# A sparse graph attention kernel: part of the single-edge product moved from VectorE to ScalarE

## The chip, the cores and the metric

The kernel runs on one core of a Trainium2 chip as one program. The metric is the device time of that program in microseconds (us). A core has five engines that run side by side, each through its own queue of instructions in order: TensorE (PE; its weight loads are shown as PEld), VectorE (DVE), ScalarE (ACT), GpSimd (POOL) and SyncE (SP). An instruction that must wait for another engine holds up everything behind it in its own queue.

## The reference

Four graph layers over 3327 nodes with 512 features and a random, sparse adjacency matrix; each adds to its input `x` a layer of the normalized input `h = relu(layernorm(x))`. Layers 0, 2 and 3 are graph attention with 8 heads of 64, layer 1 is a mean over neighbours with linear maps. Layer 3, cut to what matters (0 and 2 differ in normalization and the last function):

```python
hp = jnp.einsum('nd,hdf->hnf', h, W)                     # per head
f_src = jnp.einsum('hnf,hf->hn', hp, a_src)
f_dst = jnp.einsum('hnf,hf->hn', hp, a_dst)
e = jax.nn.leaky_relu(f_src[:, :, None] + f_dst[:, None, :], 0.2)
e = jnp.where(adj[None] > 0, e, -9e15)
out = jnp.einsum('hij,hjf->hif', jax.nn.softmax(e, axis=-1), hp)
x = x + elu(out)                                          # layer 0: batch norm and relu
```

## The kernel before

The kernel first turns the adjacency matrix into lists of neighbours, then runs four stages one after another. The three attentions share the function `attend`. It works through 52 groups of 64 target nodes, two groups to a block of 128. The blocks are taken from both ends of the list, so a block of heavy groups is followed by a block of light ones (`ls.order`).

For each node of a table, one row holds the 8 heads' projected values, each of 64 numbers and a factor (65 in all, already scaled by an exponential), and 8 more numbers T. The softmax is taken apart so that the weight of an edge is max(r, T), with r from the target and T from the source; no exponential is left in the loop.

`PLAN` (line 53) says for each group how many chunks of 128 source rows it has: dense and mixed ones, in which each source may have many targets of the group, and chunks of single edges, in which each of the 128 rows belongs to one edge. `Lists.units` (line 585) cuts these into units: up to two chunks (`SLOTS`) for the first kind, up to three (`UNIT`) for single edges. A group with six chunks of single edges has two units of three, one with five a unit of three and one of two, one with four two of two, one with three a single unit of three. The plan has 7 groups with six, 10 with five, 21 with four and 14 with three.

Work of a unit of slots: VectorE makes `mx` (the maximum, line 1581) and `wgt` (times the mask, line 1585), of 128 x 1024 for two chunks; TensorE multiplies `wgt` with the rows into the accumulator `facc` (line 1616).

Work of a unit of single edges, chunk by chunk: TensorE picks r of each edge's target (`r_of`, `pick`, line 1515) with a matrix of edges; VectorE sums its three parts (`summed`, line 1523), takes the maximum with T (line 1568) and multiplies all rows of the unit by the weights into `vw` (line 1571: 128 x 1560 for three chunks, 128 x 1040 for two). TensorE multiplies `vw` with a matrix of ones and zeros, `ones_of`, into `facc` (line 1605), chunk by chunk, with the `pick` of a later unit after the first chunk.

ScalarE's work in `attend`, in the order of its queue at unit i:
- `early(i)`: in attention 0 it copies the turned edge matrix to `edges` (`kept`, line 1502), on which a later `pick` waits, and makes masks out of bits that VectorE has cut out (`on`, line 1461): `mask` for the next unit, if that is one of slots (line 1483), and `ones_of` with its mask (lines 1478, 1479) for a unit of single edges further on. In attentions 2 and 3 it only casts `ones_of` (line 1481).
- `later()`: the generators of groups that have ended go one step each. In this order, a step per unit: ScalarE copies `facc` to `sums` (line 1419); VectorE takes the reciprocal `rd` (line 1425); ScalarE multiplies eight heads' parts by it (line 1432, eight instructions, into `bn_y` in attention 0 and `fhp` in the others). In attentions 2 and 3, after the second group of a block, `fin_e` and `fin_x` follow on ScalarE (lines 1656, 1658) and two instructions on VectorE (lines 1662, 1663). In attention 0 the sums of the batch norm run beside: GpSimd subtracts (`bn_d`, line 1715), ScalarE squares (line 1711), TensorE adds up.

TensorE, VectorE and ScalarE keep the order in which the code issues their instructions (`manual_schedule`); GpSimd, which gathers the rows (line 1342), is ordered by the scheduler. `vw` has 2 buffers in attention 0 and 3 in the others, the gathered rows `rows_e` 5 and 6, `facc` 2.

Of the kernel before, what the change touches and what calls it, by code (L numbers as in the profile page):

```python
# [23 lines left out]
F32 = mybir.dt.float32  # L24
# [9 lines left out]
ALU = mybir.AluOpType  # L34
# [5 lines left out]
P = 128  # L40
H = 8
F = 64
# [28 lines left out]
UNIT = 3  # L71
# [1233 lines left out]
def sparse(ctx: ExitStack, tc: tile.TileContext, t: dict, out: bass.AP, WA, ls, cs, idx, rdeg, bias, wx_dram, first):  # L1305
# [5 lines left out]
    nc = tc.nc  # L1311
# [35 lines left out]
    def attend(layer, table, r_dram, r3, finish, tick=lambda: None, home=None, beside=None, edges=None):  # L1347
# [14 lines left out]
        with tc.tile_pool(name=f"fatt{layer}", bufs=2) as ap, tc.tile_pool(  # L1362
            name=f"facc_ps{layer}", bufs=2, space=PSUM
        ) as aps, tc.manual_schedule(engines={ET.PE, ET.DVE, ET.Activation}):
            loaded, ones_of, st_of, found, w_of, rrs, rbs, accs, ends, over = {}, {}, {}, {}, {}, {}, {}, {}, [], []
            ahead = 2

            def fetch(j):
                if j < len(groups):
                    rr = ap.tile([2, H * GB], F32, name="r_two", tag="r_two", bufs=2)  # L1370
                    nc.sync.dma_start(rr, r_dram[groups[j], :, :, :].rearrange("t h i -> t (h i)"))
                    rrs[j] = rr

            def spread(j):


                if j < len(groups):
                    rb = aps.tile([P, H * GB], F32, name="r_bc", tag="r_bc", bufs=1)
                    nc.tensor.matmul(rb, ones[0:2, :].bitcast(F32R), rrs.pop(j).bitcast(F32R), start=True, stop=True)
                    rbs[j] = rb.rearrange("p (h i) -> p h i", i=GB)  # L1380
# [57 lines left out]
            def later():  # L1438
                for e in list(ends):
                    if next(e, 0) == 0:  # L1440
                        ends.remove(e)
                tick()

            def load(i):

                if i < len(units):
                    _, _, e, rows, _, _, _, _ = units[i]
                    if e:
                        gi = ap.tile([P, UNIT, width], I32, name="rows_e", tag="rows_e", bufs=5 if layer == 0 else 6)
                    else:  # L1450
                        gi = ap.tile([P, SLOTS, width], I32, name="rows_s", tag="rows_s", bufs=4 if layer == 0 else 5)
                    loaded[i] = gi
                    take(gi, table, rows)
# [31 lines left out]
            def turned(i):  # L1485

                if layer == 0 and i < len(units) and units[i][2]:
                    _, g, _, rows, _, _, _, _ = units[i]
                    u = g % PG
                    mine = slice(u * GB, (u + 1) * GB)  # L1490
                    st = st_of[i] = aps.tile([P, UNIT, P], F32, name="st_ps", tag="st_ps", bufs=1)
                    for k in range(len(rows)):
                        nc.tensor.matmul(st[mine, k, :], ones_of[i][:, k, :], cs["ident"], start=True, stop=True)
# [12 lines left out]
            def pick(i):  # L1506

                if i < len(units) and units[i][2]:
                    _, g, _, rows, s0, _, _, _ = units[i]
                    b, u = divmod(g, PG)  # L1510
                    mine = slice(u * GB, (u + 1) * GB)
                    st = st_of.pop(i) if layer == 0 else edges[mine, s0 : s0 + len(rows), :]
                    re = found[i] = aps.tile([P, UNIT, 3 * H], F32, name="r_of", tag="r_of", bufs=1)
                    for k in range(len(rows)):
                        nc.tensor.matmul(re[:, k, :], st[:, k, :], r3[mine, b, :], start=True, stop=True)  # L1515

            def summed(i):

                if i < len(units) and units[i][2]:
                    n, re = len(units[i][3]), found.pop(i)  # L1520
                    mx = aps.tile([P, SLOTS, H, GB], F32, name="w_of", tag="mx", bufs=1)
                    w = w_of[i] = mx[:, 0, :UNIT, :H]
                    nc.vector.tensor_reduce(w[:, :n], re[:, :n].rearrange("p k (t h) -> p k h t", h=H), AX.X, ALU.add)  # L1523
# [8 lines left out]
            def due(i):  # L1532

                return [k for k in range(max(i + 1, 0), i + ahead + 2) if k < len(units) and k - lead[k] == i]

            def early(i):

                for k in due(i - 1):
                    kept(k)
                for k in due(i):  # L1540
                    masks(k, bits(k))

            def parts(i):

                if layer == 2 and i < EPARTS:
                    for u in range(PG):
                        mine = slice(u * GB, (u + 1) * GB)
                        cut = slice(i * ls.used[u] // EPARTS, (i + 1) * ls.used[u] // EPARTS)
                        nc.sync.dma_start(edges[mine, cut, :], edges_dram[mine, cut, :])
# [10 lines left out]
            for i, (j, g, e, rows, s0, begins, stops, last_slots) in enumerate(units):  # L1560
                n, m0 = len(rows), rows[0][0]
                gt = loaded.pop(i).bitcast(F32)
                T = gt[:, :n, H * (F + 1) : ROW]
                load(i + AHEAD)
                parts(i + 1)
                if e:
                    w = w_of.pop(i)
                    nc.vector.tensor_tensor(w[:, :n], w[:, :n], T, ALU.max)
                    vw = ap.tile([P, UNIT, H, F + 1], F32, name="vw", tag="vw", bufs=2 if layer == 0 else 3)
                    full = [P, n, H, F + 1]  # L1570
                    nc.vector.tensor_tensor(  # L1571
                        vw[:, :n],
                        gt[:, :n, : H * (F + 1)].rearrange("p k (h x) -> p k h x", x=F + 1),
                        w[:, :n].unsqueeze(3).to_broadcast(full),
                        ALU.mult,
                    )
                else:
                    mk = mask[:, m0 : m0 + n, :]
                    full = [P, n, H, GB]
                    mx = aps.tile([P, SLOTS, H, GB], F32, name="mx", tag="mx", bufs=1)  # L1580
                    nc.vector.tensor_tensor(  # L1581
                        mx[:, :n], rbs[j].unsqueeze(1).to_broadcast(full), T.unsqueeze(3).to_broadcast(full), ALU.max
                    )
                    wt = ap.tile([P, SLOTS, H, GB], F32, name="wgt", tag="wgt", bufs=2 if layer == 0 else 3)
                    nc.vector.tensor_tensor(wt[:, :n], mx[:, :n], mk.unsqueeze(2).to_broadcast(full), ALU.mult)  # L1585
                summed(i + 1)
                early(i)
                if begins:
                    fetch(j + 2)
                    acc = aps.tile([P, BANK], F32, name="facc", tag="acc")  # L1590
                    accs[g] = acc

                def others():
                    pick(i + ahead)
                    if last_slots:
                        spread(j + 1)

                for k in range(n):
                    if k == 1:
                        others()  # L1600
                    f, l = begins and k == 0, stops and k == n - 1
                    if e:
                        by = vw[:, k].rearrange("p (q v) x -> p v q x", v=PG)
                        for v in range(PG):
                            nc.tensor.matmul(  # L1605
                                accs[g][v * GB : (v + 1) * GB, :sw].rearrange("p (q x) -> p q x", x=F + 1),
                                ones_of[i][:, k, :],
                                by[:, v],
                                start=f,
                                stop=l,  # L1610
                            )
                        continue
                    for q in range(hq):
                        for v in range(PG):
                            h = q * PG + v
                            nc.tensor.matmul(  # L1616
                                accs[g][v * GB : (v + 1) * GB, q * (F + 1) : (q + 1) * (F + 1)],
                                wt[:, k, h, :],
                                gt[:, k, h * (F + 1) : (h + 1) * (F + 1)],
                                start=(f and q == 0),  # L1620
                                stop=(l and q == hq - 1),
                            )
                if n == 1:
                    others()
                ones_of.pop(i, None)
                for k in due(i):
                    turned(k)
                later()
                if stops:
                    ends.append(ending(g))  # L1630
# [353 lines left out]
```

## Time and profile before

| | |
|---|---|
| device time, median of 4 runs | 2322.55 us (2319.12 to 2326.47) |
| the profiled execution: time, span of the trace | 2328.36 us, 2326.6 us |
| busy: PE, PEld | 1854.1 us (80%), 1044.1 us (45%) |
| busy: DVE, ACT, POOL | 1703.4 us (73%), 1100.0 us (47%), 1153.2 us (50%) |
| DMA | 561.86 MB, 241 GB/s on average |
| `vw` of attentions 0, 2 and 3: first and last | 370.6 and 2304.0 us |
| instructions of line 1571 | 270: 114 of 128 x 1560, 156 of 128 x 1040 |

A row of the profile names the line, the engine, the operation, what it writes and reads, its shape and its count, then busy us and the mean ns of one. In a list of waits, "A <- B" says that A's engine sat idle until B was done; the last numbers are the us in total, the times and the longest. A timeline row starts with its start and its length in us; in brackets stands the idle time ahead of it and what ended it. Neighbouring small instructions of one engine overlap in part, so the distance from start to start, not the length, is what one costs. Lines are those of the kernel before unless said otherwise.

### The profile page before, as it was taken

The page shows a single profiled execution, that of the slowest core. Times are in us where ns is not written, and L with a number is a line of the kernel's source. Part 1 is how long each engine was busy: PE and PEld are TensorE (multiplying, and loading weights), DVE is VectorE, ACT ScalarE, POOL GpSimd, SP SyncE. Part 2 cuts the span into 40 slices and gives each one's busy share as a digit, 9 for nine tenths or more (in the row PEclk, how much of TensorE's full clock was granted, in tenths as well). Part 3 has the DMA queues.
Part 4 walks back from the last instruction along what each step waited for, and adds up shares of the span by engine and source line. Part 5 has one row for each costly group of instructions (what it writes and reads, how often), then busy time and mean ns, then how long its engine had stood idle before and what let it go on. Part 6 is the DMA issues. An engine that isn't in the chain of part 4 may idle for free. (4 is left out here: it accounts for less than half of the span.)

```text
span 2326.6 us, 42809 instructions
## 1 busy us (share of the span) xinstructions
PE 1854.1 (80%) x14843; PEld 1044.1 (45%) x14843; DVE 1703.4 (73%) x3056; ACT 1100.0 (47%) x4124; POOL 1153.2 (50%) x1205
## 2 busy tenths in 40 slices
PE   4899576777888599899999857888888767777775
PEld 3655244454555244233333345555444444444442
DVE  5466977998889890255555568888777659999996
ACT  3566112555666553223333204678886713444544
POOL 0000024668777200677777356655555136776772
PEclk9789777999999899999999958998997967887777
DMA  8687157897889473888888698877777358888883
GB/s 312 248 289 278 33 198 264 291 297 245 272 263 297 146 276 114 270 256 258 267 263 257 195 299 252 263 231 242 243 244 224 104 220 270 261 285 264 281 279 112
DMA packets 204943, 561.86 MB, mean 241 GB/s; under 512 B 36985, under 2 KB 42745, under 8 KB 201392
## 3 DMA queue, kind: packets, MB, share of 16 engines
q0 software_dynamic: 93120, 327.86, 45.3%
q1 hardware_dynamic: 111600, 231.20, 28.6%
q8 instruction: 120, 1.97, 0.4%
q14 instruction: 103, 0.84, 0.1%
HBM read 496.07 MB, written 62.86 MB: 240 GB/s over the span
## 5 line engine op out<-in xcount | busy, mean ns | idle before, releaser
L1342 POOL DMA_INDIRECT rows_e<-table,idx x654 | 625.4, 956 | 670.4 <-DMA rows_s<-table 326.1
L1605 PE MATMUL facc<-vw,ones_of 128*64 128x260 f32 x2616 | 447.1, 457 | 84.8 <-DVE vw L1571 68.4
L1616 PE MATMUL facc<-rows_s,wgt 128*64 128x65 f32 x7200 | 351.7, 251 | 195.1 <-DVE wgt L1585 133.7
L1616 PEld LDWEIGHTS facc<-rows_s,wgt 128*64 128x64 f32 x7200 | 297.6, 160 | 302.6 <-DVE wgt L1585 162.6
L1571 DVE TENSOR_TENSOR vw<-rows_e,w_of 128x1040 f32<-128x1040 f32 (+1 forms) x270 | 395.7, 1466 | 9.3
L1342 POOL DMA_INDIRECT z_rows<-z_dram,idx x291 | 278.9, 959 | 231.3 <-DMA z_dram<-z_out 132.2
L1342 POOL DMA_INDIRECT rows_s<-table,idx x219 | 210.0, 959 | 212.9 <-PE facc L1616 134.5
L1581 DVE TENSOR_TENSOR mx<-r_bc,rows_s 128x1024 f32<-128x1024 f32 (+1 forms) x255 | 280.5, 1100 | 41.5 <-DMA rows_s<-table 27.8
L1432 ACT ACTIVATE fhp<-sums,rd 64x64 f32<-64x64 f32 x816 | 215.6, 334 | 185.7 <-DVE rd L1425 182.6
L1585 DVE TENSOR_TENSOR wgt<-mx,mask 128x1024 f32<-128x1024 f32 (+1 forms) x255 | 280.3, 1099 | 25.5 <-ACT mask L1483 9.0
L1605 PEld LDWEIGHTS facc<-vw,ones_of 128*64 128x64 f32 x2616 | 195.0, 156 | 223.1 <-issue 90.0
L1866 PE MATMUL sage_acc<-z_rows,z_mask 128*64 128x512 f32 x622 | 164.2, 604 | 14.3 <-DMA z_rows<-z_dram,idx 13.4
L1817 DVE TENSOR_TENSOR s_o<-n_ps,sage_b 128x512 f32<-128x512 f32 x26 | 18.0, 692 | 167.2 <-PE n_ps L1814 167.2
L1849 ACT CAST z_mask<-mask 128x128 f32<-128x128 uint8 (+1 forms) x201 | 51.2, 287 | 161.1 <-PE sage_acc L1866 158.6
L1419 ACT COPY sums<-facc 128x260 f32<-128x260 f32 x153 | 56.2, 367 | 136.7 <-PE facc L1605 135.6
L739 PE MATMUL wh_ps<-fWt,hT 128*128 128x512 f32 x208 | 115.5, 707 | 0.0
L1523 DVE TENSOR_REDUCE w_of<-r_of 128x16 f32<-128x48 f32 (+1 forms) x270 | 61.4, 227 | 65.8 <-PE r_of L1515 40.3
L1432 ACT ACTIVATE bn_y<-sums,rd 64x64 f32<-64x64 f32 x408 | 107.7, 334 | 2.6 <-DVE rd L1425 1.0
L1814 PE MATMUL n_ps<-fWx,bn_y 128*128 128x512 f32 x208 | 97.4, 611 | 0.0
L1866 PEld LDWEIGHTS sage_acc<-z_rows,z_mask 128*64 128x64 f32 x622 | 45.7, 137 | 115.0 <-issue 82.7
L921 PE MATMUL p_wh<-fWt,hT 128*128 128x512 f32 x208 | 96.1, 606 | 0.3 <-ACT hT L916 0.3
L1789 PE MATMUL z_ps<-fWx,bn_y 128*128 128x512 f32 x208 | 95.8, 606 | 0.6 <-ACT bn_y L1784 0.6
(252 smaller groups left out, 2832.0 us busy)
## 6 DMA issues: line engine op xcount, KB each, us to landing
adj_i<-in_adj SPq DMA_DIRECT2D x26, 1664.0 KB
rows_s<-table SPq DMA_DIRECT2D x46, 528.0 KB
table<-v_row SPq DMA_DIRECT2D x78, 264.0 KB
rows_s<-table SPq DMA_DIRECT2D x62, 264.0 KB
rows_s<-table SPq DMA_DIRECT2D x23, 632.0 KB
fin_x<-fx SPq DMA_DIRECT2D x52, 256.0 KB
rows_e<-table,idx POOLq DMA_INDIRECT x654
rows_s<-table SPq DMA_DIRECT2D x31, 316.0 KB
```

The costliest lines, as they stand in the source:

```text
L739: nc.tensor.matmul(wh, hT[:, kc, :], self.Wt[:, kc, :], start=(kc == 0), stop=(kc == KC - 1))
L921: nc.tensor.matmul(wh, hT[:, kc, :], self.Wt[:, kc, :], start=(kc == 0), stop=(kc == KC - 1))
L1342: nc.gpsimd.indirect_dma_start(out=dst, out_offset=None, in_=src[:, :], in_offset=bass.IndirectOffsetOnAxis(ap=idx[:, k : k + 1], axis=0))
L1432: nc.scalar.mul(hp[o0 : o0 + GB, h * F : (h + 1) * F], sm[mine, q, 0:F], rd[mine, q, :])
L1571: nc.vector.tensor_tensor(vw[:, :n], gt[:, :n, : H * (F + 1)].rearrange("p k (h x) -> p k h x", x=F + 1), w[:, :n].unsqueeze(3).to_broadca ...
L1581: nc.vector.tensor_tensor(mx[:, :n], rbs[j].unsqueeze(1).to_broadcast(full), T.unsqueeze(3).to_broadcast(full), ALU.max)
L1585: nc.vector.tensor_tensor(wt[:, :n], mx[:, :n], mk.unsqueeze(2).to_broadcast(full), ALU.mult)
L1605: nc.tensor.matmul(accs[g][v * GB : (v + 1) * GB, :sw].rearrange("p (q x) -> p q x", x=F + 1), ones_of[i][:, k, :], by[:, v], start=f, stop=l,
L1616: nc.tensor.matmul(accs[g][v * GB : (v + 1) * GB, q * (F + 1) : (q + 1) * (F + 1)], wt[:, k, h, :], gt[:, k, h * (F + 1) : (h + 1) * (F + 1)],
L1789: nc.tensor.matmul(ps, y[:, c, kc * P : (kc + 1) * P], Wx[:, 1, kc, :], start=(kc == 0), stop=(kc == KC - 1))
L1814: nc.tensor.matmul(ps, y[:, b, kc * P : (kc + 1) * P], Wx[:, 0, kc, :], start=(kc == 0), stop=(kc == KC - 1))
L1866: nc.tensor.matmul(acc[u * GB : (u + 1) * GB, :], m, z, start=f, stop=l)
```

## The change

In attentions 0 and 3, in a unit with three chunks of single edges, VectorE takes the maximum of the third chunk by itself into a new tile `w_last` (128 x 8, two buffers), then the maximum and the product of the first two chunks as before. ScalarE multiplies the third chunk's rows by the weights, head by head: eight instructions of 128 x 65, each with a column of `w_last` as its factor per partition. They stand ahead of `early(i)` and `later()` of the unit in ScalarE's queue. Units with two chunks and all units of attention 2 stay as they were. The file grows by two lines, so lines behind the change have numbers higher by two.

```diff
                 if e:
-                    w = w_of.pop(i)
-                    nc.vector.tensor_tensor(w[:, :n], w[:, :n], T, ALU.max)
+                    w, d = w_of.pop(i), n - (layer != 2 and n == UNIT)
+                    if d < n:
+                        ws = ap.tile([P, H], F32, name="w_last", tag="w_last")
+                        nc.vector.tensor_tensor(ws, w[:, d], T[:, d], ALU.max)
+                    nc.vector.tensor_tensor(w[:, :d], w[:, :d], T[:, :d], ALU.max)
                     vw = ap.tile([P, UNIT, H, F + 1], F32, name="vw", tag="vw", bufs=2 if layer == 0 else 3)
-                    full = [P, n, H, F + 1]
-                    nc.vector.tensor_tensor(
-                        vw[:, :n],
-                        gt[:, :n, : H * (F + 1)].rearrange("p k (h x) -> p k h x", x=F + 1),
-                        w[:, :n].unsqueeze(3).to_broadcast(full),
-                        ALU.mult,
-                    )
+                    full = [P, d, H, F + 1]
+                    V = gt[:, :n, : H * (F + 1)].rearrange("p k (h x) -> p k h x", x=F + 1)
+                    if d < n:
+                        for h in range(H):
+                            nc.scalar.mul(vw[:, d, h, :], V[:, d, h, :], ws[:, h : h + 1])
+                    nc.vector.tensor_tensor(vw[:, :d], V[:, :d], w[:, :d].unsqueeze(3).to_broadcast(full), ALU.mult)
```

## The prediction

> **What bounds the kernel now.** I read the page's slices first: in attention 0 and attention 3 VectorE (DVE) is the fullest engine. I then asked for the busy time of each engine in a stretch of each (columns: stretch, length, busy us of PE, PEld, DVE, ACT and POOL with instruction counts, granted TensorE clock, DMA share, GB/s).
>
> ```profile
> 365.00:790.00 425.00, 335.66 (x3850) 216.53 (x3851) 378.33 (x643) 247.00 (x827) 291.29 (x298) 0.96 0.83 267
> 1910.00:2306.00 396.00, 296.87 (x3327) 186.78 (x3325) 371.25 (x524) 172.48 (x586) 259.23 (x270) 0.80 0.83 261
> ```
>
> VectorE is busy 378 of 425 us and 371 of 396 us; ScalarE (ACT) 247 and 172. So VectorE sets the pace and ScalarE has room on average. What it waits for counts as much as its room. From the waits of ScalarE in 350 to 785 us and, below, in 1880 to 2310 us (who <- for whom: us, times, longest):
>
> ```profile
> ACT mask L1483 <- DVE on L1461: 86.3, 38, 12.4
> ```
>
> ```profile
> ACT fhp L1432 <- DVE rd L1425: 172.1, 50, 6.1
> ```
>
> ScalarE idles because VectorE has not yet written what it reads. It can't use that room for anything that also starts from a VectorE result of the same unit; the new work does exactly that.
>
> **What the change removes and adds.** By the plan, 7 groups have six chunks of single edges (two units of three), 10 have five (3+2), 14 have three: 14 + 10 + 14 = 38 units of three per attention, 76 in the two. The groups, shapes kept apart:
>
> ```profile
> L1571 DVE TENSOR_TENSOR vw<-rows_e,w_of 128x1560 f32<-128x1560 f32 x114 | 202.8, 1779 | 3.9
> L1571 DVE TENSOR_TENSOR vw<-rows_e,w_of 128x1040 f32<-128x1040 f32 x156 | 192.9, 1237 | 5.4
> L1432 ACT ACTIVATE bn_y<-sums,rd 64x64 f32<-64x64 f32 x408 | 107.7, 334 | 2.6 <-DVE rd L1425 1.0
> ```
>
> *VectorE.* The product goes from 1560 to 1040 elements: 1.779 - 1.237 = 0.54 us less. The maximum for 128x8 is new; the nearest small independent rows, a reduction at 2062.09 and a reciprocal at 2062.22, start 0.13 us apart. Net 0.41 us per unit, 38 x 0.41 = 15.6 us per attention, 31 us if every microsecond counted. Bounds: 0.54 (the new maximum free) to 0.32 (it costs the 0.22 us by which a dependent maximum holds back the product, 2062.34 to 2062.56), so 24 to 41 us in all.
>
> *ScalarE.* Eight scalings of 128x65 with a per-partition factor. The nearest row is L1432, also SBUF to SBUF with such a factor: eight in a row take 2.14 us (0.267 us from start to start). The other near row, L987 (128x64, from PSUM), takes 1.74 us for eight at 1446.99 and 1.67 at 1460.96. I take 2.15, keep 1.7 as the low bound and 8 x 0.334 = 2.67 (no overlap) as the high one. 38 x 2.15 = 82 us per attention: 329 of 425 and 254 of 396. Room on average.
>
> The Trainium skill, "ScalarE: Activation LUTs", section "What ACT_TABLE_LOAD costs", gives an ACTIVATE with one pointer operand 186 + 93 + 0.833 N ns, 93 ns of it overlapped back to back; for N = 65 that would be an estimated 0.24 us each and 1.92 us a unit. The same page, "Rules for kernel authors", speaks against the change: plain multiplies belong on VectorE. By that rule alone the total would rise; the busy rows above, with VectorE the full engine, say the opposite.
>
> *Order.* In the changed kernel's instruction order nothing else moves, except a few of POOL's gathers past each other and past its bn_d subtractions. TensorE waits for ScalarE only at the third chunk's matmuls. But the scalings stand at the start of a unit in ScalarE's queue. Behind them stand: the copy of edges (L1502) that TensorE's pick waits for between its chunks; the mask (L1483) that wgt of a following unit of slots waits for; eight L1432 of an earlier group; the copy of sums (L1419) that VectorE's reciprocal rd waits for; and in attention 3 fin_e and fin_x, which L1662 waits for. VectorE runs in order, so each of these, if late, stops it.
>
> **Walks.** I moved the rows of the timeline by hand: the third chunk's 0.41 us off VectorE, 2.15 us into ScalarE from 0.1 us after the new maximum, in the changed order. Attention 0, the worst group (six chunks), VectorE and then ScalarE before:
>
> ```profile
> 432.81 0.19 DVE L1568 TENSOR_TENSOR w_of<-w_of,rows_e 128x24 f32<-128x24 f32 x1
> 433.03 1.78 DVE L1571 TENSOR_TENSOR vw<-rows_e,w_of 128x1560 f32<-128x1560 f32 x1
> ...
> 435.33 0.18 DVE L1568 TENSOR_TENSOR w_of<-w_of,rows_e 128x24 f32<-128x24 f32 x1
> 435.55 1.78 DVE L1571 TENSOR_TENSOR vw<-rows_e,w_of 128x1560 f32<-128x1560 f32 x1
> ...
> 439.10 1.22 DVE L1585 TENSOR_TENSOR wgt<-mx,mask 128x1024 f32<-128x1024 f32 x1 [0.42 <-ACT mask L1483]
> ```
>
> ```profile
> 435.44 0.36 ACT L1478 ACTIVATE ones_of<-on 128x192 f32<-128x192 uint16 x1 [3.30 <-DVE on L1461]
> ...
> 436.10 2.13 ACT L1432 ACTIVATE bn_y<-sums,rd 64x64 f32<-64x64 f32 x8
> 438.26 0.47 ACT L1502 CAST edges<-st_ps 64x384 bf16<-64x384 f32 x1
> 438.75 0.31 ACT L1483 ACTIVATE mask<-on 128x128 uint8<-128x128 uint16 x1
> ```
>
> After: scalings 433.0 to 435.15, ones_of and its copy to 435.9, the eight L1432 to 438.05, the second unit's scalings to 440.2, edges to 440.7, mask to 441.0. VectorE, 0.8 us ahead, is ready for wgt at about 438.2 and gets it at 441.05: 2.9 us idle, 1.95 us later than now. Not all are like this. From 392 to 505 us (20 units of three) I find, in the change of VectorE's clock: groups of six -0.3, +0.3, +1.85, +0.95, 0, +1.45, 0; the three pairs of three-chunk groups between them 0 (+0.1, -0.1, 0): together **+4.2 us**. The other 18 units: pairs of three-chunk groups again 0; of the five-chunk groups four walked (521, 531, 565 and 589 us) give 0, +1, 0, 0, since rd already waits for sums there; +1 for all. Attention 0: **+5**.
>
> Attention 3 has no masks to make, so ScalarE's queue is shorter. The place that hurts is the second of two three-chunk groups (VectorE's rows, then ScalarE's, now):
>
> ```profile
> 1986.37 0.19 DVE L1568 TENSOR_TENSOR w_of<-w_of,rows_e 128x24 f32<-128x24 f32 x1
> ...
> 1990.88 0.17 DVE L1425 RECIPROCAL rd<-sums 128x4 f32<-128x4 f32 x1
> ```
>
> ```profile
> 1986.45 2.14 ACT L1432 ACTIVATE fhp<-sums,rd 64x64 f32<-64x64 f32 x8 [4.58 <-DVE rd L1425]
> 1988.61 0.38 ACT L1419 COPY sums<-facc 128x260 f32<-128x260 f32 x1
> ```
>
> Now sums is ready 1.9 us before rd. After, scalings (2.15), eight L1432 (2.15) and sums (0.4) end 4.9 us after the new maximum; VectorE reaches rd 4.1 us after it: 0.9 us idle, at six such pairs 5.4 us. The eight L1432 between two units of scalings, with fin behind, hold VectorE at L1662 1.8 us at 2003.48 and 0.4 at 2037.36: 2.2. The last pair ends the kernel: fin_x at 2306.97 comes 2.2 us later, uncovered. Five-chunk groups keep their gain. 15.6 - 5.4 - 2.2 - 2.2 = **-5.8 us**.
>
> **Sum.** +5 - 5.8 = -0.8. I add +2 for what I did not walk: POOL's bn_d waits for ScalarE's bn_y already (19.4 us, 9 times), gathers queue behind it, and bn_y comes later; nearest rows: nothing, or as much again. So +1 us on the profiled execution: 2328.36 (span 2326.6 and 1.8 around it) to 2329.5. That execution lies 5.8 above the median; the same +1 on 2322.55 gives **2324 us**. A difference under 0.3% (7 us) can't be told from none here.
>
> **Rivals.**
> - *Bursts absorbed (faster).* If eight scalings take 1.7 us and the queue of ScalarE is shorter than I drew, each of some 35 stalls loses 0.45 us or more, 16 us: 2308; with everything hidden 2322.55 - 31 = 2291. For: ScalarE's idle 172 us; against: that idle time ends with VectorE's own rows.
> - *ScalarE becomes the pace in attention 0 (slower).* In a three-chunk group it would have sums 0.4, L1432 2.15, scalings 2.15, edges 0.5, mask and ones 1.0 and a share of the squares 0.3: 6.5 us, against 5.2 for VectorE there. From the point at which the heavy groups between no longer let it catch up (a backlog over one unit, some 2.5 us), each of the 14 loses 1.3 - 0.4 = 0.9 us and each of the 7 groups of six loses like the one at 439 us (2): +27 at most, +12 to +18 likely, less 3 in attention 3: 2335.
> - *It does not do what it says.* If the third chunk were waited for as a whole tile, TensorE would lose up to 2 us at 76 units. The waits in its order speak against it.
>
> **Numbers.** Forecast (within 0.3%) 0.45; bursts absorbed 0.24; ScalarE the pace 0.29; tile wait 0.02. Its own range 2317 to 2331; with the others 2306 to 2342. Faster 0.24, same 0.45, slower 0.31.
>
> **What will show it.** Product rows all of 1040; 608 scalings near 0.33 us each, 0.27 apart; ScalarE's busy time up by 160 us, VectorE's from 1703 to about 1675. VectorE's waits for mask (7.4 us in attention 0) and for sums (4.6 and 0.6) at least doubled if I am right; unchanged with a shorter attention 3 by 14 us if the first rival holds; attention 0 longer by over 10 us if the second. I am wrong if TensorE's pick or POOL's gathers, not VectorE's waits for ScalarE, carry the difference.

## The result, and the profile after

| | before | after |
|---|---|---|
| device time, median | 2327.47 us (65 runs, 2319.12 to 2334.96) | 2330.46 us (42 runs, 2320.79 to 2340.38) |
| ratio | | 1.0015, 95% interval 1.0008 to 1.0022 |
| profiled execution, span | 2328.36, 2326.6 us | 2329.76, 2328.0 us |

So 3 us slower. The interval leaves out 1, so the loss is real, but it is inside the 0.3% (7 us) in which the prediction would not tell a difference from none. The profiled execution was forecast at 2329.5 us. The forecast median, 2324 us, is 6.5 us below the measured one, mostly because the four runs on which it stood lie 4.9 us below the 65 of the table. The ratios below leave out single executions that were far longer than the rest, one of 2662 us in e2 and one of 8748.5 us in e6 among them. The first eight experiments below (e1 to e8) ran while every kernel, the one before too, took 12% longer (2601 to 2620 us), for a reason that is not known; the last four (e9 to e12), on the chip of e5 to e8, had 2327.6 us for the kernel before, so each is compared only with the kernel before of its own group.

Everything that the diff says is there. The groups of the changed kernel (line, engine, tile, shape, count, then busy us, mean ns of one, and the idle time ahead):

```profile
L1577 ACT ACTIVATE vw<-rows_e,w_last 128x65 f32<-128x65 f32 x608 | 153.7, 336 | 60.9 <-DVE w_last L1570 41.9 <-issue 12.8 <-DMA rows_e<-table,idx 3.8
L1578 DVE TENSOR_TENSOR vw<-rows_e,w_of 128x1040 f32<-128x1040 f32 x232 | 286.9, 1237 | 8.2
L1578 DVE TENSOR_TENSOR vw<-rows_e,w_of 128x1560 f32<-128x1560 f32 x38 | 67.6, 1779 | 1.3
L1570 DVE TENSOR_TENSOR w_last<-w_of,rows_e 128x8 f32<-128x8 f32 x76 | 12.4, 163 | 1.4
```

The 76 products of 1560 in the two attentions are now 1040; the 38 left belong to attention 2. VectorE is busy 1676.7 us in all (1703.4 before), ScalarE 1245.7 (1100.0).

Where the time went shows best between two fixed marks: from the start of the first product `vw` of an attention to the end of its last one. Busy time of each engine there, first before (attention 0, attention 3), then after:

```profile
370.58:788.45 417.87, 329.03 (x3758) 210.89 (x3754) 373.01 (x631) 243.79 (x816) 290.03 (x297) 0.96 0.83 268
1917.86:2305.80 387.94, 291.63 (x3243) 182.07 (x3242) 364.54 (x516) 172.28 (x586) 259.23 (x270) 0.81 0.83 261
```

```profile
372.05:798.12 426.07, 333.25 (x3741) 213.94 (x3738) 360.88 (x669) 312.71 (x1110) 290.56 (x297) 0.95 0.82 263
1923.84:2304.03 380.19, 289.38 (x3241) 181.63 (x3240) 350.29 (x554) 243.16 (x881) 258.33 (x270) 0.81 0.85 267
```

The third number with a count in brackets is VectorE. In attention 0 it has 12.1 us less to do (373.01 to 360.88), yet the stretch is 8.2 us longer: its idle time, length less busy, goes from 44.9 to 65.2 us. In attention 3 it has 14.3 us less to do, its idle time grows from 23.4 to 29.9, and the stretch is 7.8 us shorter. From the start of the last product to the end of the program (the tail) it was 22.6 us and is 25.2: 2.6 more. Between the attentions (from attention 0's last product to attention 3's first, by starts) it was 1131.2 us and is 1127.0; the same kernel's second profile, e9, has 1130.9, so most of that difference is the noise of an execution. The three executions without the new work on ScalarE and of this pace (before, e10, e12) have 1131.2, 1129.8 and 1129.9 us there, the three with it (after, e9, e11) 1127.0, 1130.9 and 1127.0: whether these stages give back one or two us of attention 0's loss stays open.

What VectorE now waits for, changed kernel, 350 to 785 us and then 1880 to 2310 us (us, times, longest):

```profile
DVE wgt L1587 <- ACT mask L1483: 20.1, 20, 2.7
DVE rd L1425 <- ACT sums L1419: 7.8, 13, 1.6
DVE on L1461 <- ACT ones_of L1478: 2.5, 4, 0.9
```

```profile
DVE rd L1425 <- ACT sums L1419: 7.0, 7, 3.2
DVE fin_x L1664 <- ACT fin_x L1660: 2.4, 2, 1.3
```

They were 7.4, 4.6 and 0.6, then 0.6 and 1.1: VectorE's new idle time is nearly all waiting for ScalarE (in attention 0 these three grew by 17.8 us and a wait of 1.3 us for `edges` is new; the idle time grew by 20.3). The wait of 3.2 us for sums belongs to the tail, not to the stretch.

The worst group of six, which the prediction moved by hand, as it came out in the changed kernel (VectorE, then ScalarE; start, length):

```profile
438.72 1.23 DVE L1583 TENSOR_TENSOR mx<-r_bc,rows_s 128x1024 f32<-128x1024 f32 x1
442.64 1.22 DVE L1587 TENSOR_TENSOR wgt<-mx,mask 128x1024 f32<-128x1024 f32 x1 [2.70 <-ACT mask L1483]
```

```profile
434.97 2.03 ACT L1577 ACTIVATE vw<-rows_e,w_last 128x65 f32<-128x65 f32 x8 [0.86 <-DVE w_last L1570]
437.07 0.36 ACT L1478 ACTIVATE ones_of<-on 128x192 f32<-128x192 uint16 x1
437.46 0.35 ACT L1479 CAST mask<-ones_of 128x192 uint8<-128x192 f32 x1
437.72 2.13 ACT L1432 ACTIVATE bn_y<-sums,rd 64x64 f32<-64x64 f32 x8
439.88 2.03 ACT L1577 ACTIVATE vw<-rows_e,w_last 128x65 f32<-128x65 f32 x8
441.93 0.47 ACT L1502 CAST edges<-st_ps 64x384 bf16<-64x384 f32 x1
442.30 0.31 ACT L1483 ACTIVATE mask<-on 128x128 uint8<-128x128 uint16 x1
```

ScalarE has room on average (312.7 of 426 us), but from 434.97 it works through seven items without a pause, and the one that VectorE needs is the last.

### The profile page after: what moved, and what is told of

It is laid out like the page before. It is cut to its first block, busy times and chain, and to the rows that moved or that the text cites. A ratio compares the mean times of both kernels' runs of the same rounds, so it can differ in the third digit from the quotient of the medians.

```text
span 2328.0 us, 43559 instructions
## 1 busy us (share of the span) xinstructions
PE 1849.6 (79%) x14843; PEld 1043.9 (45%) x14843; DVE 1676.7 (72%) x3132; ACT 1245.7 (54%) x4732; POOL 1152.9 (50%) x1205
## 5 line engine op out<-in xcount | busy, mean ns | idle before, releaser
L1607 PE MATMUL facc<-vw,ones_of 128*64 128x260 f32 x2616 | 452.6, 455 | 72.3 <-DVE vw L1578 32.5
L1578 DVE TENSOR_TENSOR vw<-rows_e,w_of 128x1040 f32<-128x1040 f32 (+1 forms) x270 | 354.5, 1313 | 9.5
L1432 ACT ACTIVATE fhp<-sums,rd 64x64 f32<-64x64 f32 x816 | 215.5, 334 | 86.9 <-DVE rd L1425 83.5
L1577 ACT ACTIVATE vw<-rows_e,w_last 128x65 f32<-128x65 f32 x608 | 153.7, 336 | 60.9 <-DVE w_last L1570 41.9
L1432 ACT ACTIVATE bn_y<-sums,rd 64x64 f32<-64x64 f32 x408 | 107.7, 334 | 1.9 <-DVE rd L1425 0.2
```

What stands on the lines that cost most here:

```text
L1432: nc.scalar.mul(hp[o0 : o0 + GB, h * F : (h + 1) * F], sm[mine, q, 0:F], rd[mine, q, :])
L1577: nc.scalar.mul(vw[:, d, h, :], V[:, d, h, :], ws[:, h : h + 1])
L1578: nc.vector.tensor_tensor(vw[:, :d], V[:, :d], w[:, :d].unsqueeze(3).to_broadcast(full), ALU.mult)
L1607: nc.tensor.matmul(accs[g][v * GB : (v + 1) * GB, :sw].rearrange("p (q x) -> p q x", x=F + 1), ones_of[i][:, k, :], by[:, v], start=f, stop=l,
```

## The experiments

| | what | ratio to the kernel before, beside it | 95% |
|---|---|---|---|
| e1, e6 | attention 3 only | 1.0041; 1.0063 | 1.0012 to 1.007; 1.003 to 1.0095 |
| e2 | attention 0 only | 1.0058 | 1.0029 to 1.0087 |
| e3, e7 | third chunk's product left out | 1.0008; 1.000 | 0.9973 to 1.0044; 0.9965 to 1.0035 |
| e4 | ScalarE's work added, VectorE not relieved | 1.0098 | 1.0059 to 1.0137 |
| e8 | scalings later in ScalarE's queue | 1.0073 | 1.0035 to 1.011 |
| e9 | the change again | 1.0012 | 0.9998 to 1.0027 |
| e10 | second chunks of slots left out on TensorE | 1.0006 | 0.9993 to 1.0019 |
| e11 | the same, with the change | 1.0026 | 1.001 to 1.0042 |
| e12 | the same, third chunk left out | 0.9878 | 0.986 to 0.9896 |

The theory: in these two attentions VectorE sets the pace, and its relief is eaten by its waits for ScalarE's queue. The rivals: something else (gathered rows, TensorE) sets the pace, so that the relief was worth little to begin with; or ScalarE's amount of work counts, wherever it stands.

**e1 and e2: one attention at a time.** The condition `layer != 2` becomes `layer == 3` or `layer == 0`.

```diff
-                    w, d = w_of.pop(i), n - (layer != 2 and n == UNIT)
+                    w, d = w_of.pop(i), n - (layer == 3 and n == UNIT)
```

> The third chunk goes to ScalarE in attention 3 alone. Theory (VectorE sets the pace, and what it saves is lost again where it waits for ScalarE's queue): attention 3 keeps about what the trace of the changed kernel shows between the first and the last product, 7 us, less some 2.5 us at the uncovered end, so 4 to 6 us faster than before (ratio near 0.998). Rival (give-back: the shift of 10 us made in attention 0 is worked off by the stages behind it, whatever they contain, as 4 us of it were in the untouched attention 2): with no shift there is nothing to work off, and the time is that of before, within 1 us, or 2.5 us longer for the end.

> The third chunk goes to ScalarE in attention 0 alone. Theory: attention 0 is longer by 8 to 9 us as in the changed kernel, and nothing gives it back: 2334 to 2336 us (ratio near 1.0035). Rival (give-back in the stages behind): 2327 to 2331 us, with attentions 2 and 3 visibly shorter than before.

e1 took 2631.05 us beside 2620.09: 11 us slower where I expected 4 to 6 faster. e2 took 2634.92, 14.8 us slower where I expected 8 to 9. For attention 3 alone the theory missed.

**e3: relief without the burden.** VectorE leaves the third chunk out, nobody makes it, and TensorE takes the second chunk's product again.

```diff
+                    w, d = w_of.pop(i), n - (layer != 2 and n == UNIT)
+                    nc.vector.tensor_tensor(w[:, :d], w[:, :d], T[:, :d], ALU.max)
...
-                        by = vw[:, k].rearrange("p (q v) x -> p v q x", v=PG)
+                        by = vw[:, min(k, d - 1)].rearrange("p (q v) x -> p v q x", v=PG)
```

> Leaves work out: the product of the third chunk is made by no engine, TensorE takes the second chunk's product twice instead, and the separate maximum is gone too. Theory: VectorE sets the pace in both attentions, 0.54 us saved at 76 units, 41 us; nearly all of it is seen: 30 to 41 us faster. Rival (the feed: gathers by GpSimd, busy 85% of the time with its gaps, or TensorE set the pace close behind VectorE): less than 15 us faster, with VectorE's waits for the gathered rows or for r_of grown by the rest.

2617.76 us beside 2620.09: nothing gained, within 0.4%, by some 40 us less of VectorE's work (76 units of 0.54 us). Under the conditions of that job the rival holds: VectorE did not set the pace.

**e4: the burden without the relief.** ScalarE scales the third chunk into a spare tile, and VectorE makes all three chunks.

```diff
+                        spare = ap.tile([P, H, F + 1], F32, name="spare", tag="spare", bufs=1)
+                        for h in range(H):
+                            nc.scalar.mul(spare[:, h, :], V[:, d, h, :], ws[:, h : h + 1])
+                        d = n
```

> Adds work: ScalarE makes its eight scalings of the third chunk, at the same place in its queue, into a tile that nobody reads, while VectorE makes the maximum apart and multiplies all three chunks as before. Theory: VectorE loses 0.13 us at 76 units for the extra maximum (10 us) and waits for mask, sums and fin_x as in the changed kernel, less some since it comes to them 0.5 us later: 18 to 28 us slower. Rival (the queue of ScalarE costs little; what the changed kernel loses comes from TensorE waiting for the third chunk): 8 to 12 us slower, with VectorE's waits for mask and sums as before the change.

2642.94 us, 1.0098: 22.9 us slower, inside the theory's 18 to 28. The loss of e1 and e2 together, 1.0041 times 1.0058, is 1.0099, as large as that of the added work alone, and e3 (1.0008) says that the relief was worth nothing there. But the added work is ScalarE's scalings and VectorE's small maximum, and the waits do not say how it costs time: in attention 0 (350 to 885 us) VectorE waits 17.5 us for the mask, and 25.0 in the kernel before at that pace (e5, on another chip). The theory's wait is not shown in this job.

**e5 to e8: what set the pace there.** A second job came out as slow, so the kernel before was profiled in it.

> The kernel before, profiled once more, as the control for the traces. On a chip of the pace of the first runs (some 2327 us) the starts of VectorE's products should again span 416 us in attention 0 and 386 us in attention 3 (370.6 to 786.7 and 1917.9 to 2304.0 in the first profile); how far they miss by chance is the noise of one execution, which every reading of a shift of a few us has to stand above. On a chip of the pace of the slower runs (some 2620 us) it gives the profile of before that those four kernels lack; there I expect VectorE's longest waits to be for TensorE's r_of and for gathered rows, not for ScalarE.

TensorE's waits in e5, whole run:

```profile
PE facc L1616 <- issue: 129.9, 172, 3.0
PE facc L1605 <- DVE vw L1571: 62.4, 47, 5.3
PE facc L1605 <- issue: 25.1, 52, 1.1
PE r_of L1515 <- issue: 14.1, 11, 4.5
```

and the first 12 matmuls of a unit of slots in it, where all 16 took 0.69 us when undisturbed (timeline of TensorE; the other four follow after another 1.08 us):

```profile
444.23 0.55 PE L1616 MATMUL facc<-rows_s,wgt 128*64 128x65 f32 x7
445.28 0.22 PE L1616 MATMUL facc<-rows_s,wgt 128*64 128x65 f32 x1 [0.50 <-issue]
446.03 0.24 PE L1616 MATMUL facc<-rows_s,wgt 128*64 128x65 f32 x1 [0.53 <-issue]
447.41 0.35 PE L1616 MATMUL facc<-rows_s,wgt 128*64 128x65 f32 x3 [1.14 <-issue]
```

"issue" is time in which an engine waits for nothing that the trace shows. In the first profile of this kernel the first of these rows has 5.1 us in 9 times:

```profile
PE facc L1616 <- issue: 5.1, 9, 1.1
```

Here TensorE stands still in the middle of a unit, over and over, and VectorE waits for TensorE: its row `w_of` waits 45.0 us for `facc` (L1616) in 32 times, a wait that the first profile does not have. TensorE is not alone in it: time put down to "issue" is 77.2 us on VectorE and 185.9 on ScalarE in e5, 0.3 and 32.5 in the first profile. In e5 another 102.5 us of VectorE's waits end by "remote", a release that the trace has no instruction for; the first profile has none of them. VectorE is busy 65% of the span instead of 73%. I expected its longest waits to be for `r_of`, for rows and not for ScalarE; for `r_of` it waited 53.5 us, for `mask` 25.0, so that was only half right.

> ScalarE takes the third chunk in attention 3 only. Theory (VectorE sets the pace; attention 0 loses by waits for ScalarE, attention 3 gains): on a chip of the pace of 2327 us, 4 to 6 us less than before, ratio 0.9975 to 0.9983; attention 0 spans 416 us from first to last product as before, attention 3 379 as with the whole change. Rival (attention 3's shorter span was the chance of one execution): within 1.5 us of before, attention 3 near 386. On a chip of the pace of 2620 us, where VectorE is not the pace: no gain, 1.002 to 1.005 as in the first run.

> Leaves out the third chunk's product in attentions 0 and 3 altogether (no scalings; TensorE takes the second chunk's product again in its place), so it has VectorE's full relief without ScalarE's new work. Theory (VectorE sets the pace in both stages): on a chip of the pace of 2327 us, 76 units of 0.54 us, 30 to 41 us less than before, ratio 0.982 to 0.987. Rival (the rows gathered or TensorE set the pace, so the relief was worth little and ScalarE's new work cost little): less than 15 us, 0.994 or above. On a chip of the pace of 2620 us: 0.997 to 1.004 as in the first run.

e6 repeats e1 (1.0063) and e7 repeats e3 (1.000); the last sentence on e7 had 0.997 to 1.004 for such a job, that on e6 1.002 to 1.005, which was too low. By the starts of its products attention 3 spans 459.2 us in e5, 459.6 in e6 and 450.9 in e7, one execution each, so even the full relief of 20 us is worth some 8 there. In e6 the changed attention is no longer than in e5, and from its last product's start to the end it is 24.9 us instead of 22.6: where e6 loses the rest is not shown. What made TensorE stop was not found.

> The whole change, but the eight scalings stand behind the unit's copy of edges, its ones_of and its mask in ScalarE's order instead of ahead of them. Theory (it is the place in ScalarE's queue that stops VectorE): in attention 0 VectorE's wait for the mask falls from 20.1 us to about 8 as before, TensorE's wait for the third chunk rises from 8.8 to 20 or more, and attention 0 is 3 to 5 us shorter than with the change as it was: ratio to before 0.9995 to 1.0005. Rival A (it is the amount of work on ScalarE, wherever it stands): 1.001 to 1.002, unchanged. Rival B (TensorE, then late at the third chunk, holds up the buffers of products): 1.003 or more. Attention 3 has no masks and edges to make and should stay as with the change (379 us from first to last product).

```diff
                 early(i)
+                if e and d < n:
+                    for h in range(H):
+                        nc.scalar.mul(vw[:, d, h, :], V[:, d, h, :], ws[:, h : h + 1])
```

(the loop is taken out ahead of `early(i)`). 2623.18 us, 1.0073. The number is on rival B's side, but all three ranges were set for a change that costs 1.0015; in such a job the change would cost 1.0099 by e1 and e2 (an estimate, from another chip), which is inside the interval of e8, so the ratio does not decide. TensorE's waits in attention 0 of e8 (350 to 885 us), and VectorE's:

```profile
PE facc L1607 <- ACT vw L1589: 50.8, 33, 4.2
```

```profile
DVE wgt L1584 <- ACT mask L1483: 32.5, 22, 2.7
DVE rd L1425 <- ACT sums L1419: 23.7, 19, 2.5
```

In e2, with the scalings ahead and on another chip, these three were 15.9, 19.6 and 6.4. Moving the scalings back did not free the mask (the theory's number was about 8), TensorE waited longer for the third chunk, and VectorE longer for `sums`. By the starts of its products attention 0 spans 517.5 us in e8 and 503.7 in e5, 13.8 more; in the job of e2 it spans 517.4 in e2 and 508.3 in e1, where it is unchanged, 9.1 more. So the move did not help, by one execution of each and in such a job only; with VectorE as the pace it was not tried.

**e9: the change again, under the first conditions.**

> The change itself, unaltered, next to the kernel before on the chip that this job gets. On a chip of the pace of 2327 us: 1.0015 again, with attention 0 about 9 us longer and attention 3 about 7 us shorter. On one of the pace of 2600 us, where TensorE stands still for about 1 us at a time with nothing that the trace shows to wait for, and VectorE has slack: theory (ScalarE's lateness now reaches TensorE and nothing is gained for VectorE's relief) the two halves measured alone add up, 1.004 to 1.006 each, so 1.008 to 1.012. Rival (the halves' cost was the chance of those runs, the change costs what it costs elsewhere): 1.000 to 1.003.

2329.96 us beside 2327.63. The stretches of the two attentions, as above:

```profile
370.35:796.07 425.72, 335.40 (x3741) 216.52 (x3738) 359.77 (x669) 312.08 (x1110) 290.47 (x297) 0.94 0.83 263
1925.72:2305.28 379.56, 285.15 (x3239) 179.33 (x3239) 350.36 (x554) 243.22 (x880) 258.79 (x270) 0.82 0.85 267
```

They repeat the first profile of the change within 0.7 us, and the tail is 25.2 us again. For the kernel before there is one profile of this pace, but e10 below, with the same work on VectorE, has 417.1 and 387.9 us. So +8 and -8 are no chance of one execution.

**e10 to e12: take TensorE out of the question.** To ask about VectorE on any chip, the second chunk's matmuls of a unit of slots are left out in attentions 0 and 3 (unless they end a group), in the kernel before (e10), the changed one (e11) and the one without the third chunk (e12).

```diff
+                    if layer != 2 and k and not stops:
+                        continue
                     for q in range(hq):
```

> The kernel before, with the second chunk's matmuls of a unit of slots left out in attentions 0 and 3 (where they are not the group's last), so TensorE has about 100 us less of its work with rows_s and waits for VectorE on any chip. Base for the next two. VectorE's work is the same. Theory: the span of attentions 0 and 3 falls towards VectorE's busy time (some 380 us each), on a chip of the pace of 2600 us by 40 us or more in total (ratio 0.985 or less), on one of 2327 us hardly (0.99 to 1.0). Rival (the gathered rows set the pace on the slower chips, not TensorE): less than 15 us, 0.994 or above.

> The changed kernel with the same matmuls left out as in the base before it. Theory (with VectorE the pace, attention 0 loses by waiting for ScalarE's queue and attention 3 gains): against that base, attention 0 5 to 11 us longer, attention 3 4 to 9 us shorter from first to last product, in total within 5 us, ratio between the two 0.998 to 1.003. Rival A (relief is worth its full size once VectorE is the pace, and the loss in attention 0 came by TensorE): 15 us or more below the base. Rival B (the change costs through TensorE's waits for ScalarE, whatever sets the pace): 15 us or more above the base.

> The same base with the third chunk's product left out in attentions 0 and 3 and no scalings (TensorE takes the second chunk's product again): VectorE's full relief, 0.54 us at 76 units, without ScalarE's work. Theory (VectorE the pace): 25 to 41 us below the base, ratio between the two 0.984 to 0.990. Rival (gathered rows the pace): less than 10 us below.

e10 2328.99 us, e11 2334.08, e12 2299.23. e10 has 2080 of 14843 matmuls fewer, though TensorE's busy time fell only from 1854 to 1817 us, since the others took longer (those of `vw` 482 ns instead of 457, at a lower clock, see the end); I had expected 100 us less. It stands at 1.0006 of the kernel before, which its theory for this pace and its rival both allow: those matmuls are not what bounds it. Against e10, e11 is 1.0022 by the medians (resampled runs: 0.9997 to 1.0039; 5.1 us, where the theory said within 5) and e12 0.9872 (0.9857 to 0.9889), inside the theory's ranges of the ratio and outside the rivals'. The stretches, e10, e11, e12:

```profile
373.44:790.56 417.12, 325.15 (x2854) 193.60 (x2853) 368.52 (x631) 243.09 (x816) 292.07 (x297) 0.88 0.83 268
1918.53:2306.42 387.89, 269.03 (x2337) 153.84 (x2335) 364.18 (x516) 172.33 (x586) 260.12 (x270) 0.75 0.83 261
```

```profile
371.95:798.85 426.90, 323.46 (x2854) 195.00 (x2853) 361.08 (x669) 312.54 (x1111) 291.51 (x297) 0.90 0.82 262
1924.58:2304.49 379.91, 269.85 (x2331) 154.37 (x2329) 350.12 (x554) 243.24 (x880) 260.27 (x270) 0.75 0.84 266
```

```profile
372.23:781.42 409.19, 322.36 (x2854) 195.58 (x2853) 350.96 (x631) 242.97 (x814) 290.48 (x297) 0.89 0.84 273
1910.03:2277.10 367.07, 263.36 (x2329) 150.07 (x2327) 343.37 (x516) 171.37 (x584) 258.89 (x270) 0.75 0.86 276
```

Read the lengths. In attention 3 the relief alone takes 20.8 us off (387.89 to 367.07), all of VectorE's 20.8 us of busy time: there every microsecond of VectorE counts. With ScalarE's scalings, 8.0 are left: of the 12.8 lost between e12 and e11, 6.8 are VectorE's own new work (350.12 less 343.37, nearly all of it the small maximum) and only 6.1 new idle time. In attention 0 the relief alone takes off only 7.9 of 17.6 us, and with the scalings the stretch is 9.8 us longer than with neither. Between e12 and e11 that is 17.7 us: 7.6 are idle time, 6.1 the small maximum, and 3.5 a longer `on`, which the last section explains and which differs from execution to execution. So splitting the maximum cost about as much as ScalarE's lateness did on top of e12. Why the relief alone was worth so little in attention 0 is read from VectorE's waits of e12 (350 to 785 us):

```profile
DVE wgt L1581 <- ACT mask L1483: 15.6, 14, 3.5
DVE on L1461 <- DMA rows_e<-table,idx: 9.7, 6, 3.1
DVE rd L1425 <- ACT sums L1419: 6.5, 9, 1.4
```

In e10 they are 8.6, 5.8 and 4.4. The mask comes late even without new work on ScalarE, which fits that VectorE reaches it sooner; gathered rows likewise.

## Why the prediction was right, point by point

- **The relief of VectorE** was sized 0.41 us a unit, 15.6 an attention; its busy time fell by 12.1 (attention 0) and 14.3 (attention 3), 0.32 and 0.38 a unit, at and above my low bound of 0.32. The failed part is the new maximum: I took 0.13 us, it takes 0.18 to 0.20 from its start to the next one's (434.77 to 434.97). Attention 0 got less because `on` (line 1461) was busy 57.2 us there instead of 55.2.
- **The scalings** were sized 2.15 us for eight and take 2.05 (439.88 to 441.93). Busy time per scaling is 0.253 us (153.7 over 608). From the Trainium skill, "ScalarE: Activation LUTs", section "What ACT_TABLE_LOAD costs", the estimate was 0.24 and 1.92, about as far below as the L1432 row was above.
- **Attention 0**, forecast +5 us, came +8.2 (e9 +7.9). By the starts of the products the change had cost 4.6 us (e9 4.2) at the product that began at 502 us before, where my walk of the first 20 units ended with 4.2. The three groups of six that were to cost +1.85, +0.95 and +1.45 cost 1.7, 0.7 and 1.1. So the walked part was right and the failed step is "+1 for all" of the other 18 units: they cost 4.2 (8.7 at the last product's start, e9 8.4). Nearly half of that (1.9) is the last unit, a place that I had not walked: VectorE there waits 3.48 us for the mask, 1.56 before, since ScalarE's queue holds eight L1432, a square (L1713) and eight scalings ahead of it:

```profile
789.87 2.14 ACT L1432 ACTIVATE bn_y<-sums,rd 64x64 f32<-64x64 f32 x8
792.03 0.63 ACT L1713 ACTIVATE bn_d<-bn_d 128x512 f32<-128x512 f32 x1
792.57 2.01 ACT L1577 ACTIVATE vw<-rows_e,w_last 128x65 f32<-128x65 f32 x8
794.60 0.47 ACT L1502 CAST edges<-st_ps 64x384 bf16<-64x384 f32 x1
795.10 0.26 ACT L1483 ACTIVATE mask<-on 128x64 uint8<-128x64 uint16 x1
```

- **The worst group**: 2.9 us of waiting forecast at wgt, 2.70 measured.
- **Attention 3**, forecast 15.6 less 7.6, so -8.0 ahead of the tail, came -7.8 (e9 -8.4). That it fits so well is luck: the relief was 14.3 instead of 15.6, and VectorE's idle time grew by 6.5 us instead of 7.6. The waits stood where the walk had them. The wait for sums behind two three-chunk groups was forecast at 0.9 and is 0.64 at each of the six pairs, 3.8 in all instead of 5.4; of the two at `fin_x` one came, 1.3 us instead of 2.2 for both. One of the six:

```profile
1994.81 0.18 DVE L1425 RECIPROCAL rd<-sums 128x4 f32<-128x4 f32 x1 [0.64 <-ACT sums L1419]
```

- **The tail**, forecast +2.2 uncovered, came +2.6. The last sums hold VectorE 3.16 us, 0.64 before:

```profile
2307.19 0.18 DVE L1425 RECIPROCAL rd<-sums 128x4 f32<-128x4 f32 x1 [3.16 <-ACT sums L1419]
```

- **+2 for POOL.** The delay came, and was made up. With the end of attention 0 (350 to 885 us) POOL's wait for `bn_y` went from 19.4 to 25.0 us (e9 24.4), and the mean of the batch norm starts 11.16 us behind the start of the last product instead of 9.18 (11.16 in e9 and e11 too, 10.25 in e10), first before, then after:

```profile
795.85 0.69 DVE L1720 SCALAR_TENSOR_TENSOR bn_mean<-bn_shift,bn_mean 128x512 f32<-128x512 f32 x1 [4.65 <-ACT bn_mean L1692]
808.04 0.69 DVE L1722 SCALAR_TENSOR_TENSOR bn_mean<-bn_shift,bn_mean 128x512 f32<-128x512 f32 x1 [5.60 <-ACT bn_mean L1694]
```

But 155 us behind the last product, at the first `s_o`, nothing of these 2.0 us is left (0.0, e9 0.2), so in the total the reserve was not needed.

- **The total.** That +1 came so near (+1.4 on the profiled execution, +3.0 and +2.3 by the medians) is partly luck. By the starts of the products the two attentions and the tail make +4.1 (8.7 - 7.2 + 2.6; e9 +3.2), and in the first profile stretches that the change does not touch gave 2.7 back. Attention 0 was 3 us too cheap in the forecast, and the reserve of 2 stood in for it.
- **The rivals.** Bursts absorbed: no, the waits for mask and sums grew instead of staying (of those that were to double, mask in attention 0 and sums in attention 3 did, sums in attention 0 went from 4.6 to 7.8). ScalarE as the pace in attention 0: it needed over 10 us there, and +8.2 lies nearer to that than to my 5, so the length alone does not settle it. But ScalarE still idles 113 of 426 us there, of which 83.5 (350 to 785 us) end with VectorE's rows, and the shift does not pile up from group to group: it falls from 7.9 us at 565 to 4.3 at 582. TensorE waiting for a whole tile: it waits for ScalarE's `vw` 9 times in attention 0, 8.8 us in all, and 13 times in attention 3, 15.0 us, not 2 us at each of 76 units.

What stays open: whether the change in attention 3 alone is faster by some 5 us under the first conditions (an estimate from e9: -8.4 in the stretch, +2.6 in the tail). It was measured only at the pace of 2600 us, where it cost 0.4 and 0.6%. How much of attention 0's loss is the place of the scalings in ScalarE's queue, and how much their amount, was not separated at the pace of 2327 us. None of these kernels beat the kernel before with the whole computation done.

## What to carry to other kernels

Before moving work to an engine with room, list what already stands in that engine's queue behind the place where the new work goes, and who waits for it: the room on average (113 us of 426 in attention 0, with the new work in it) was real and still not usable in bursts of 2 us. Test the worth of the relief by itself, with the work left out and nobody doing it: here it was worth all of its time in one stage and under half in another that looked nearly as full. Count the small instruction that the split adds: 0.16 us at each of 38 units took 6.1 us of a relief of 20.6. Walk the last unit of a stage as well as the worst one: it cost 1.9 us in attention 0 and 2.6 at the end of the kernel.

## What the runs showed of the hardware

The same kernel on the same chip took 2601 us in one job and 2327.6 in a later one. Its VectorE groups were equal (1225 ns for `wgt` of 128x1024 in both profiles); TensorE had gaps without a cause in the trace, and DMA moved 216 instead of 241 GB/s. Under those conditions a change that is nearly neutral elsewhere was slower in each of its halves, so a difference of 0.5% holds only for the conditions in which it was measured.

VectorE's `on` (line 1461, 128 x 128 of 16 bits) takes 0.28 us in the median, but longer where it runs into GpSimd's subtraction `bn_d` (line 1715, 1.28 us):

```profile
732.89 0.95 DVE L1461 TENSOR_TENSOR on<-rows_e,fbit 128x128 uint16<-128x128 uint16 x1
```

GpSimd's row beside it runs from 732.40 to 733.68. In attention 0 of all six profiles at 2300 to 2330 us, every `on` of over 0.5 us overlaps such a subtraction. Its busy time there varies from 50.6 (e10) to 57.4 us (e11), so a few us of VectorE's busy time in attention 0 are a matter of where the two meet.

Leaving out matmuls lowered the granted TensorE clock at an unchanged total time: over the span 0.869 to 0.884 in the runs of the kernel before and 0.848 to 0.862 in those of e10, in attention 3 0.81 before and 0.75 in e10. The Trainium skill, "TensorE: Matmul & The Clock Gate", section "Part 1: The HAM clock gate", says that the throttled clock is the default and that activity releases it; these numbers agree in direction. So a low granted clock can be the mark of an idle TensorE and need not be the cause of a long run.
